# The input part of a recurrence: copied into PSUM by ScalarE in place of an identity product

## The chip, the cores and the metric

The kernel runs on one core of a Trainium2 chip. A core has TensorE (PE; its weight loads are listed apart as PEld), VectorE (DVE), ScalarE (ACT), GpSimd (POOL) and SyncE (SP), each with its own queue of instructions; they wait for each other through semaphores. Matrix products write to PSUM, which has eight banks of 512 f32 values for each of 128 partitions. The metric is the time of one execution on the device, in microseconds (us).

## What is computed

The program is a chain of graph layers and feed-forward layers over a graph of 3125 nodes with 256 features. The change lies in one of them, a recurrence over B = 1, T = 3125 steps on layer-normalised rows x:

```python
xt = jnp.swapaxes(x, 0, 1)
xi = xt @ U_i + b_i          # and xf, xg, xo
def step(carry, xs):
    h, c = carry
    xi_t, xf_t, xg_t, xo_t = xs
    i_t = jax.nn.sigmoid(xi_t + h @ V_i)
    g_t = jnp.tanh(xg_t + h @ V_c)
    o_t = jax.nn.sigmoid(xo_t + h @ V_o)
    c_new = h * c + i_t * g_t
    h_new = o_t * jnp.tanh(c_new)
    return ((h_new, c_new), h_new)
(_, _), hs = lax.scan(step, (h0, c0), (xi, xf, xg, xo))
```

The forget gate isn't used in the new cell: the old cell is multiplied by h. The layer's output is hs, and it is added to x.

## The kernel before

The method `recurrence` cuts the 3125 steps into 64 chunks of 49 (G = 2 groups, R = 32 chunks in each, L = 49 steps) and runs all chunks side by side, each from a guess of its starting state. It repeats this for ROUNDS = 5 rounds, each of which takes the chunks' starting states from the ends of the chunks before them in the round before. The first round, `round_(SKIP)`, begins at step 20 and so has 29 steps; four more rounds of 49 steps stand in a hardware loop, `For_i` (L1843). At the end a flag is set where the last two rounds still differ; any flag starts the program's second path, a general version of everything.

Before the rounds, the input part of all steps, x times U plus bias, is computed once into the SBUF tile `pre` (L1735 with target px, and L1757). One partition holds one chunk's part of one quarter of the features: 4 quarters x 32 chunks are 128 partitions, and a row of 192 values holds 64 features for each of three gates.

One step of one group is, by the names in the profile:

- L1770, `before_h`: TensorE multiplies the identity with `pre` for this step and group. This writes the input part into the PSUM tile `pz` (start=True); each group has two such tiles, in a bank each (L1760).
- L1735, `quarters`: eight products of `hist` (the transposed h of the step before, as weights) with the matrix `lstm_v`, four quarters for each of two halves of h, added in `pz`. In f32 a product is two records in the trace, so there are 16 to a step.
- L1815: ACT takes the tanh of all three gates, `z`.
- L1817 and L1821: DVE makes `ig` from z and then the new `cell`, with `hc` (h times the old cell, L1793, made a half step earlier).
- L1829: ACT takes the tanh of the cell, `tcell`.
- L1831 and L1835: DVE makes `h` and transposes it into `hist`, from which the next step's products load their weights.

The two groups are independent within a round and are written in turn, g = 0 and g = 1 for each step. A planner in the framework sets the order of instructions on each engine from its own estimates of when each is ready. `issue_after(x)` keeps what is written in its block behind x in the queue of x's engine; it adds no wait. Here it keeps each identity product behind the products of the step, those behind the previous identity product, and `hc` behind the other group's cell. The framework also places the semaphore waits. An instruction that needs more waits than it can hold gets an event-semaphore instruction ahead of it, on the same engine, for the rest.

Of the kernel before, what the change touches and what calls it, by code (L numbers as in the profile page):

```python
# [13 lines left out]
AF = mybir.ActivationFunctionType  # L14
ALU = mybir.AluOpType
AX = mybir.AxisListType
PSUM = bass.MemoryType.PSUM
# [58 lines left out]
class Net:  # L76
# [1608 lines left out]
    def recurrence(self, name, general=False):  # L1685
# [17 lines left out]
        nc, x = self.nc, self.x  # L1703
# [3 lines left out]
        G, L = GROUPS, CHUNK  # L1707
        T = G * R * L
        with ExitStack() as ctx:
# [15 lines left out]
            pre = c.tile([P, G, L, W], F32, name="pre")  # L1725
# [5 lines left out]
            def quarters(pz, stationary, moving, start, stop):  # L1731
                for q in range(Q):
                    s = stationary[q] if isinstance(stationary, list) else stationary
                    m = moving if len(moving.shape) == 2 else moving[:, q, :]
                    made = nc.tensor.matmul(  # L1735
                        pz[q * R : (q + 1) * R, :], s, m,
                        start=start, stop=stop, tile_position=(0, q * R),
                    )
                return made.ins

            with ExitStack() as inner:
                wk = self.pool(inner, name + "projwork", 3)
                xt = self.pool(inner, name + "projx", 1).tile([P, KD, NP], F32, name="xt")
                psum = self.pool(inner, name + "projps", 4, space=PSUM)
# [7 lines left out]
                for g in range(G):  # L1752
                    for s in range(L):
                        pz = psz.tile([P, W], F32, name="px", padded_shape=[P, 512])
# [2 lines left out]
                        nc.vector.tensor_add(pre[:, g, s, :], pz, bs)  # L1757
            with ExitStack() as inner:
                wk = self.pool(inner, name + "work", 3)
                psum = [self.pool(inner, f"{name}ps{g}", 2, space=PSUM) for g in range(G)]  # L1760
                pst = self.pool(inner, name + "pst", 1, space=PSUM)
                hall = c.tile([P, KD, NP], F32, name="hall")
                nc.gpsimd.memset(hall[:, :, T:], 0.0)
                nc.vector.memset(ends, 0.0)
                nc.vector.memset(start_t, 0.0)
                nc.vector.memset(hist[:, :, L - 1], 0.0)

                def before_h(g, s):
                    pz = psum[g].tile([P, W], F32, name="pz", padded_shape=[P, 512])
                    made = nc.tensor.matmul(  # L1770
                        pz, self.ident, pre[:, g, s, :], start=True, stop=False
                    )
                    return pz, made.ins

                def round_(begin=0):

                    first = wk.tile([P, 2, J], F32, name="first")
                    celt = wk.tile([P, KD, R], F32, name="celt")
                    nc.vector.tensor_copy(start_t[:, 0, :, 1:], hist[:, 1, L - 1, :, 0 : R - 1])
                    nc.vector.transpose(celt.rearrange("p k r -> p (k r)"), ends[:, 1, 1, :])  # L1780
                    nc.vector.tensor_copy(start_t[:, 1, :, 1:], celt[:, :, 0 : R - 1])
                    for i in range(2):
                        nc.vector.transpose(
                            first[:, i, :], start_t[:, i].rearrange("p k r -> p (k r)")
                        )
                    h = [first[:, 0, :], ends[:, 0, 0, :]]
                    cell = [first[:, 1, :], ends[:, 1, 0, :]]
                    ht = [start_t[:, 0], hist[:, 0, L - 1]]
                    hc = [None] * G

                    def carried(g):
                        to = wk.tile([P, J], F32, name=f"hc{g}")
                        nc.vector.tensor_mul(to, h[g], cell[g])  # L1793
                        return to


                    pz = []
                    for g in range(G):
                        tile, last = before_h(g, begin)
                        pz.append(tile)  # L1800
                    for s in range(begin, L):
                        for g in range(G):
                            with self.tc.issue_after(last):
                                for k in range(KD):
                                    made = quarters(
                                        pz[g], ht[g][:, k, :], vs[:, k], False, k == KD - 1
                                    )
                            last, following = made, None
                            if s + 1 < L:
                                with self.tc.issue_after(made):  # L1810
                                    following, last = before_h(g, s + 1)
                            if hc[g] is None:
                                hc[g] = carried(g)
                            z = wk.tile([P, W], F32, name=f"z{g}")
                            nc.scalar.activation(z, pz[g], AF.Tanh)  # L1815
                            ig = wk.tile([P, J], F32, name=f"ig{g}")
                            nc.vector.scalar_tensor_tensor(  # L1817
                                ig, z[:, 0:J], 1.0, z[:, 2 * J :], op0=ALU.add, op1=ALU.mult
                            )
                            now = wk.tile([P, J], F32, name=f"cell{g}")  # L1820
                            made = nc.vector.scalar_tensor_tensor(  # L1821
                                now, hc[g], 0.5, ig, op0=ALU.mult, op1=ALU.add
                            )
                            cell[g], hc[g] = now, None
                            if g == 0 or s + 1 < L:
                                with self.tc.issue_after(made.ins):
                                    hc[1 - g] = carried(1 - g)
                            tcell = wk.tile([P, J], F32, name=f"tcell{g}")
                            nc.scalar.activation(tcell, cell[g], AF.Tanh, scale=0.5)  # L1829
                            h[g] = wk.tile([P, J], F32, name=f"h{g}")  # L1830
                            nc.vector.scalar_tensor_tensor(  # L1831
                                h[g], z[:, J : 2 * J], 1.0, tcell, op0=ALU.add, op1=ALU.mult
                            )
                            ht[g] = hist[:, g, s]
                            nc.vector.transpose(ht[g].rearrange("p k r -> p (k r)"), h[g])  # L1835
                            pz[g] = following
                    for g in range(G):
                        for i, now in enumerate((h[g], cell[g])):
                            nc.vector.tensor_sub(moved[:, i, g, :], now, ends[:, i, g, :])
                            nc.vector.tensor_copy(ends[:, i, g, :], now)  # L1840

                round_(SKIP)
                with self.tc.For_i(0, (G * R if general else ROUNDS) - 1, 1):  # L1843
                    round_()

                halls = [
                    hall[:, k, :T].rearrange("p (b g s) -> p g s b", g=G, s=L) for k in range(KD)
                ]
                for b in range(0, R, R // 2):
                    cut = slice(b, b + R // 2)  # L1850
                    for g in range(G):
                        nc.vector.tensor_scalar(
                            halls[0][:, g, :, cut], hist[:, g, :, 0, cut], 0.5, None, op0=ALU.mult
                        )
                        nc.scalar.mul(halls[1][:, g, :, cut], hist[:, g, :, 1, cut], 0.5)

                last = wk.tile([P, 1], F32, name="last")
                nc.vector.tensor_reduce(last, self.ident[:, R - 1 :: R], AX.X, ALU.add)
                nc.vector.tensor_scalar(last, last, -1.0, 1.0, op0=ALU.mult, op1=ALU.add)
                nc.vector.tensor_mul(moved, moved, moved)  # L1860
                nc.vector.tensor_scalar(moved, moved, 4 * TOL * TOL, None, op0=ALU.is_le)
                nc.vector.tensor_scalar(moved, moved, -1.0, 1.0, op0=ALU.mult, op1=ALU.add)
                nc.vector.tensor_scalar(
                    moved[:, :, 1, :], moved[:, :, 1, :], last, None, op0=ALU.mult
                )
                count = wk.tile([P, 1], F32, name="count")
                nc.vector.tensor_reduce(count, moved, AX.XYZ, ALU.add)
                pc = pst.tile([P, 512], F32, name="pc")
                nc.tensor.matmul(pc[:1, :1], count, self.ones[:, 0:1], start=True, stop=True)
                nc.vector.tensor_copy(self.flags[:, 4:5], pc[:1, :1])  # L1870
# [940 lines left out]
```

## Time and profile before

| what | us |
|---|---|
| median of 3 runs | 4003.65 (4002.43 to 4005.65) |
| the profiled execution | 4006.18 |
| its span, first to last instruction | 4004.5 |
| projection into `pre`, L1735 into px | 1615.8 to 1681.4 |
| first round, 29 steps | 1681.4 to 1764 |
| four rounds of 49 steps | 1764 to 2343 |
| one identity product, two records | 0.59 |
| the 16 records of a step's products | 0.86 |
| `z`, 128x192 | 0.33 |
| `tcell`, 128x64 | 0.26 |

In a group's line, the number after x is the count of records, then come the busy time and the mean of one in ns, then the engine's idle time just before them and what ended most of it. In the timeline the columns are start, duration, engine, line and operation, then out<-in with the shape. Square brackets give the idle time before the instruction and what ended it. In the windows the columns are the stretch, its length, the busy time of PE, PEld, DVE, ACT and POOL with counts, the granted share of the TensorE clock, the share of the DMA engines and GB/s.

### The profile page before, as it was taken

How to read it: one execution, taken by the hardware profiler on the slowest of the kernel's cores; microseconds unless marked ns; L12 is line 12 of the kernel's file. 1: busy time of each engine (PE TensorE's matmuls, PEld its weight loads, DVE VectorE, ACT ScalarE, POOL GpSimd, SP SyncE). 2: the span in 40 equal slices, each digit the busy share in tenths (PEclk: the TensorE clock that was granted, in tenths of full speed). 3: DMA queues.
4: the chain of work that ended last, by engine and by line, in shares of the span. 5: the costliest groups of instructions: out<-in, count | busy, mean ns of one | idle time of the engine just before them, and what ended most of it. 6: DMA issues, size and time to landing. Idle time of an engine off the chain costs nothing. (4 is left out here: it accounts for less than half of the span.)

```text
span 4004.5 us, 71406 instructions
## 1 busy us (share of the span) xinstructions
PE 3505.5 (88%) x25991; PEld 2138.1 (53%) x26079; DVE 2149.8 (54%) x7762; ACT 1171.7 (29%) x3566; POOL 1422.2 (36%) x1316
## 2 busy tenths in 40 slices
PE   4776986668898798999999979999999999899898
PEld 3343222553232476745444555555566888766687
DVE  7787997447777566677666671111256211244411
ACT  2565334243333111134333441001001322220122
POOL 2777776345787375000000021111122222222243
PEclk7677997788999899999999989999999999899999
DMA  4556343553444554000000012333464444435465
GB/s 122 160 160 191 107 115 94 163 190 108 114 124 106 137 159 125 4 2 2 2 2 2 2 30 78 94 91 92 135 183 152 118 120 121 141 110 156 118 166 122
DMA packets 366365, 422.12 MB, mean 105 GB/s; under 512 B 44076, under 2 KB 320864, under 8 KB 362295
## 3 DMA queue, kind: packets, MB, share of 16 engines
q1 hardware_dynamic: 286833, 260.46, 21.8%
q0 software_dynamic: 62224, 140.41, 13.8%
q10 hardware_dynamic: 16950, 16.54, 1.3%
q8 instruction: 217, 3.56, 0.4%
q14 instruction: 141, 1.16, 0.1%
HBM read 337.37 MB, written 82.62 MB: 105 GB/s over the span
## 5 line engine op out<-in xcount | busy, mean ns | idle before, releaser
L1952 POOL DMA_INDIRECT edge<-scored,from x720 | 853.5, 1185 | 339.7 <-issue 181.2
L1735 PE MATMUL pz<-lstm_v,hist 128*32 128x192 f32 x7120 | 384.6, 334 | 31.5 <-DVE hist L1835 8.6
L1515 PE MATMUL acc<-c,hs 128*128 128x512 bf16 (+1 forms) x2070 | 406.0, 356 | 1.6
L1535 PE MATMUL acc<-hs,c 128*128 128x512 bf16 x1192 | 394.9, 379 | 0.0
L2599 PE MATMUL ph<-xt,first 128*128 128x256 f32 (+1 forms) x1624 | 350.4, 371 | 2.7 <-DMA first<-in_f_first 1.9
L2005 ACT ACTIVATE edge<-edge,factor 128x65 f32<-128x65 f32 (+1 forms) x960 | 251.4, 349 | 316.4 <-DVE factor L2000 251.9
L1539 PE MATMUL acc<-hs,c 128*128 128x256 bf16 x1250 | 340.6, 272 | 3.0
L2617 PE MATMUL py<-w,ht 128*128 x1484 | 335.8, 380 | 0.7 <-DVE y L2622 0.7
L1515 PEld LDWEIGHTS <-hs 128*128 128x128 bf16 x2100 | 205.5, 98 | 198.9
L2599 PEld LDWEIGHTS ph<-xt,first 128*128 128x128 f32 x1624 | 291.2, 197 | 38.3 <-ACT xt L2565 2.1
L2617 PEld LDWEIGHTS py<-w,ht 128*128 128x128 f32 x1484 | 282.0, 191 | 38.9 <-issue 1.0
L1735 PEld LDWEIGHTS pz<-lstm_v,hist 128*32 128x32 f32 x7120 | 186.7, 109 | 180.1 <-DVE hist L1835 147.5
L1770 PE MATMUL pz<-pre,ident 128*128 128x192 f32 x900 | 269.8, 383 | 12.2 <-PEq L1843 12.2
L1586 POOL TENSOR_TENSOR disc<-deg,expo 128x25 f32<-128x25 f32 x1 | 4.4, 4357 | 769.7 <-DVE ends L1840 769.7
L2269 POOL DMA_INDIRECT slots<-rows,sloti x150 | 164.7, 1098 | 315.2 <-DVE rstd L340 136.8
L2607 ACT ACTIVATE ht<-ph,first 128x256 f32<-128x256 f32 (+1 forms) x406 | 160.6, 455 | 310.5 <-PE ph L2599 301.6
L971 DVE SCALAR_TENSOR_TENSOR v<-q,g1ahv,c 128x384 f32<-128x384 f32 (+1 forms) x400 | 236.9, 643 | 11.1 <-PE acc L1038 11.0
L1123 PE MATMUL acc<-g1bhv,v 128*128 128x257 f32 x850 | 204.7, 396 | 14.6 <-DVE v L971 8.4
L1770 PEld LDWEIGHTS pz<-pre,ident 128*128 128x128 f32 x900 | 136.9, 191 | 150.1 <-issue 72.0
L1815 ACT ACTIVATE z<-pz 128x192 f32<-128x192 f32 x450 | 148.6, 330 | 189.9 <-PE pz L1735 164.2
L2015 PE MATMUL edgeacc<-edge,hot 128*32 128x264 f32 (+1 forms) x1440 | 142.5, 462 | 69.1 <-DVE edge L2008 34.7
L676 PE MATMUL pa<-hi,lo 128*128 128x350 bf16 (+2 forms) x600 | 163.8, 422 | 41.7 <-DVE hi L667 34.9
(532 smaller groups left out, 5426.6 us busy)
## 6 DMA issues: line engine op xcount, KB each, us to landing
c<-ct SPq DMA_DIRECT2D x103, 640.0 KB
c<-ct SPq DMA_DIRECT2D x75, 480.0 KB
first<-in_f_first SPq DMA_DIRECT2D x29, 1158.0 KB
slots<-slots SPq DMA_DIRECT2D x159, 130.0 KB
ct<-cols SPq DMA_DIRECT2D x12, 1600.0 KB
first<-in_f_first SPq DMA_DIRECT2D x29, 642.0 KB
edge<-scored,from POOLq DMA_INDIRECT x720
first<-in_f_first SPq DMA_DIRECT2D x29, 385.0 KB
```

Source lines behind the costliest of these rows:

```text
L971: nc.vector.scalar_tensor_tensor(to, q[:, h, :w], hv[:, s, h, D // nh + 1 : D // nh + 2], cols[s], op0=ALU.max, op1=ALU.mult,)
L1123: nc.tensor.matmul(a[:, : D + 1], v[0][:, j * P : (j + 1) * P], hv[:, s, 0, : D + 1], start=(s == 0), stop=(s == NT - 1),)
L1515: self.nc.tensor.matmul(acc[f][:, : n * P], lhs, cols[s], start=(s == 0 and i == 0), stop=(s == NT - 1), skip_group_check=True,)
L1535: nc.tensor.matmul(acc[t], lhs, hs[:, s, 0:2, :].rearrange("p i d -> p (i d)"), start=start, stop=stop, skip_group_check=True,)
L1539: return nc.tensor.matmul(acc[t][:, D:], lhs, hs[:, s, 2, :], start=False, stop=stop, skip_group_check=True,)
L1735: made = nc.tensor.matmul(pz[q * R : (q + 1) * R, :], s, m, start=start, stop=stop, tile_position=(0, q * R),)
L1770: made = nc.tensor.matmul(pz, self.ident, pre[:, g, s, :], start=True, stop=False)
L1952: nc.gpsimd.indirect_dma_start(out=tile[:, g, :], out_offset=None, in_=self.rows, in_offset=bass.IndirectOffsetOnAxis(ap=index, axis=0),)
L2005: nc.scalar.mul(part, part, factor[:, g, h : h + 1])
L2269: nc.gpsimd.indirect_dma_start(out=net.slot_views[(2 * t + r) % len(net.slot_views)], out_offset=bass.IndirectOffsetOnAxis(ap=self.sloti[: ...
L2599: made = nc.tensor.matmul(ph[:, m - m0, :n, :], st["w1"][:, k * hid + m * P : k * hid + (m + 1) * P], st["xt"][:, k, :n, :], start=(k == 0 ...
L2617: nc.tensor.matmul(py[:, j, :], st["ht"][:, m, j, :], st["w2"][:, m * D : (m + 1) * D], start=(m == 0), stop=(m == nhc - 1),)
```

## The change

`before_h` no longer issues a product. ACT copies the step's slice of `pre` into `pz`, and all eight products of the step are then added to it: they were already written with start=False, and get an argument that leaves out a check of groups. The copy for step s+1 is kept behind the z of step s on ACT's queue. The products no longer stand behind the identity product of the other group but behind that group's products. Each group has three PSUM tiles for `pz` in place of two. Line numbers after L1735 shift by a few in the changed file: the copy is L1771, z L1811, ig L1816, cell L1820, tcell L1828, h L1830, the transpose L1834.

```diff
                     made = nc.tensor.matmul(
                         pz[q * R : (q + 1) * R, :], s, m,
                         start=start, stop=stop, tile_position=(0, q * R),
+                        skip_group_check=True,
                     )
...
-                psum = [self.pool(inner, f"{name}ps{g}", 2, space=PSUM) for g in range(G)]
+                psum = [self.pool(inner, f"{name}ps{g}", 3, space=PSUM) for g in range(G)]
...
                     pz = psum[g].tile([P, W], F32, name="pz", padded_shape=[P, 512])
-                    made = nc.tensor.matmul(
-                        pz, self.ident, pre[:, g, s, :], start=True, stop=False
-                    )
-                    return pz, made.ins
+                    nc.scalar.copy(pz, pre[:, g, s, :])
+                    return pz
...
                     for g in range(G):
-                        tile, last = before_h(g, begin)
-                        pz.append(tile)
+                        pz.append(before_h(g, begin))
+                    last = None
                     for s in range(begin, L):
                         for g in range(G):
-                            with self.tc.issue_after(last):
+                            with self.tc.issue_after(last) if last else nullcontext():
                                 for k in range(KD):
                                     made = quarters(
                                         pz[g], ht[g][:, k, :], vs[:, k], False, k == KD - 1
                                     )
                             last, following = made, None
-                            if s + 1 < L:
-                                with self.tc.issue_after(made):
-                                    following, last = before_h(g, s + 1)
                             if hc[g] is None:
                                 hc[g] = carried(g)
                             z = wk.tile([P, W], F32, name=f"z{g}")
-                            nc.scalar.activation(z, pz[g], AF.Tanh)
+                            made = nc.scalar.activation(z, pz[g], AF.Tanh).ins
+                            if s + 1 < L:
+                                with self.tc.issue_after(made):
+                                    following = before_h(g, s + 1)
```

## The prediction

> **What bounds the kernel now.** I read the page first (which lines are costly), then the windows around the recurrence, then the timeline of two steps, then the event-semaphore rows and the granted clock. The page:
>
> ```profile
> span 4004.5 us, 71406 instructions
> L1735 PE MATMUL pz<-lstm_v,hist 128*32 128x192 f32 x7120 | 384.6, 334 | 31.5 <-DVE hist L1835 8.6
> L1770 PE MATMUL pz<-pre,ident 128*128 128x192 f32 x900 | 269.8, 383 | 12.2 <-PEq L1843 12.2
> ```
>
> The removed line shows 270 us of TensorE time, and the recurrence (1681 to 2343 us) shows TensorE about 93% busy, as in this window, one pass of the loop (columns: PE, PEld, DVE, ACT, POOL, clock, DMA):
>
> ```profile
> 1909.50:2052.90 143.40, 133.66 (x1764) 70.89 (x1764) 100.53 (x502) 57.46 (x196) 0.00 (x0) 0.99 0.01 2
> ```
>
> That share misleads. The timeline of one full step of a group (rows of the other group are between them):
>
> ```profile
> 2041.20 0.86 PE L1735 MATMUL pz<-lstm_v,hist 128*32 128x192 f32 x16
> 2041.98 0.59 PE L1770 MATMUL pz<-pre,ident 128*128 128x192 f32 x2
> 2042.18 0.33 ACT L1815 ACTIVATE z<-pz 128x192 f32<-128x192 f32 x1 [0.33 <-PE pz L1735]
> ...
> 2042.54 0.22 DVE L1817 SCALAR_TENSOR_TENSOR ig<-z 128x64 f32<-128x64 f32 x1
> 2042.80 0.22 DVE L1821 SCALAR_TENSOR_TENSOR cell<-hc,ig 128x64 f32<-128x64 f32 x1
> ...
> 2043.12 0.26 ACT L1829 ACTIVATE tcell<-cell 128x64 f32<-128x64 f32 x1 [0.61 <-DVE cell L1821]
> ...
> 2043.41 0.23 DVE L1831 SCALAR_TENSOR_TENSOR h<-z,tcell 128x64 f32<-128x64 f32 x1 [0.24 <-ACT tcell L1829]
> 2043.50 0.33 ACT L1815 ACTIVATE z<-pz 128x192 f32<-128x192 f32 x1
> 2043.74 0.24 DVE L1835 STREAM_TRANSPOSE hist<-h 128x64 f32<-128x64 f32 x1
> 2043.91 0.18 DVE L1817 SCALAR_TENSOR_TENSOR ig<-z 128x64 f32<-128x64 f32 x1
> 2044.04 0.48 PEld L1735 LDWEIGHTS pz<-lstm_v,hist 128*32 128x32 f32 x16 [0.44 <-DVE hist L1835]
> ```
>
> Start to start: products to z 0.98, z to ig 0.36, ig to cell 0.26, cell to tcell 0.32, tcell to h 0.29, h to transpose 0.33, transpose to next products 0.30: 2.85 us, all of it one group's dependences. The products start 0.05 us after the transpose ends, in both groups, so TensorE is free then. The identity product (2041.98) runs while z, ig and cell do: it is off the path.
>
> **The price of a second wait.** Early in the first round cell to tcell takes 0.25 us, not 0.32:
>
> ```profile
> 1686.47 0.23 DVE L1821 SCALAR_TENSOR_TENSOR cell<-hc,ig 128x64 f32<-128x64 f32 x1
> 1686.72 0.26 ACT L1829 ACTIVATE tcell<-cell 128x64 f32<-128x64 f32 x1 [0.55 <-DVE cell L1821]
> ```
>
> There tcell waits on one semaphore; from the eighth step on it has an extra event-semaphore instruction that carries the wait for cell: about 0.06 us. The same holds for z, and for the transpose from step 20 of a round (0.33 against 0.26). So a step takes 2.66 us in the first seven steps, 2.77 where the transpose has one wait, 2.85 where it has two.
>
> **The change, part by part.** Orders and waits below are those of the two built programs; outside the recurrence every engine's list is the same.
>
> (a) 450 identity products leave TensorE (900 records, 269.8 us). They lie beside z and the cell arithmetic; inside a step they free nothing, since the products wait for the transpose: 0.
>
> (b) 450 copies on ACT, pre to PSUM, 128x192. Nearest rows: tcell 0.26 (128x64, SBUF) and z 0.33 (128x192, out of PSUM) below, the 128x256 SBUF activation at L1204 0.41 above. Order is z, copy, tcell, with no wait on the copy in the steps. ACT idles 0.61 us between z and tcell, so even 0.41 fits: 0. If that cover were gone, each excess would come straight onto tcell.
>
> (c) Waits. tcell's event semaphore goes (-0.06). The first product of a step now waits for the transpose, an older product and the copy, and the wait for the transpose moves to an event-semaphore instruction on TensorE:
>
> ```profile
> L1770 PEldq EVENT_SEMAPHORE  x16: 51/51/51, 1761.5 to 2204.5; - x16
> ```
>
> In the trace a weight load starts 0.053 us after the releasing DVE instruction; where such an instruction carried the wait, 0.115 (L347, L505, L1876). Queued behind it are only this burst and the other group's, which comes later anyway. So +0.06. Sum with tcell: 0. Bounds: PE's could cost 0 to 0.12, that is -0.06 to +0.06 a step.
>
> (d) Order on VectorE, which the source diff doesn't show. Before: h, transpose, then the other group's ig. After, in every step but one of a round, one group (X) has h, **ig of the other group (Y), then X's transpose**. X's transpose is queued behind an instruction that waits for Y's z, and Y's z stands behind X's tcell in ACT's queue. X's cycle becomes: z to tcell 0.36+0.26+0.26 = 0.88; tcell to Y's z 0.16 (back-to-back activations overlap, row below: seven take 1.77 us, one 0.34, so the next starts about 0.10 before the end; 0.26-0.10); z to ig 0.36; ig to transpose 0.16 (as transpose to ig, 2043.74 to 2043.91); transpose to products 0.36; products to z 0.99. Sum 2.91.
>
> ```profile
> 1199.81 1.77 ACT L2005 ACTIVATE edge<-edge,factor 128x65 f32<-128x65 f32 x7
> ```
>
> Y's own cycle, with X's transpose between its ig and cell (+0.06), gives 2.84 to 2.91 and fits in. Against 2.85: +0.06; against 2.77: +0.14; against 2.66: +0.25. First round: 22 x 0.14 + 7 x 0.25 = 4.8. Four passes of 20 x 0.14 + 29 x 0.06 = 4.5: 18.2. Sum **+23 us**. Bounds: no cost at all (the ig is always early): 0. If activations don't overlap (+0.10) and ig to transpose costs as much as ig to cell (+0.10): 3.11 a step, 22 x 0.34 + 7 x 0.45 + 4 x (20 x 0.34 + 29 x 0.26) = +68. I take the middle sum: its rows are back-to-back rows of the same engines.
>
> (e) Round starts. The two identity products ahead of the first real ones run at half clock (2054.56 to 2056.14), though start_t was ready at 2054.61; two copies on ACT take about 0.6 and then the products can go: -1.2 for the first group, about -2 for the second, four times: -8. Against that, TensorE stays at half clock until enough work fills a window; now 3.4 to 6.8 us a round, then perhaps 0 to 8 windows more at 1 us of loss each; two more, +2 a round: +8. Sum 0, bounds -8 and +30.
>
> (f) Third PSUM bank per group: no row shows a wait for a bank in the steps. 0. The Trainium skill (Perfetto Trace Analysis, Matmul Optimizations) advises to use all eight banks; by that rule a gain would be expected, by this trace none.
>
> Sum: 23 + 0. The profiled execution took 4006.18 us (span 4004.5), 2.5 above the median of the runs; on the median, 4003.65 + 22 = **4026**.
>
> **Rivals.** *The clock falls* (slower by far). Without the identity products TensorE is busy 2 x 0.86 of 2.91 us, 59%, and in the thinnest 3.4 us window 2 x 0.86 = 51%. Three windows:
>
> ```profile
> 1322.40:1325.80 3.40, 2.01 (x8) 1.24 (x8) 0.29 (x2) 1.75 (x9) 0.00 (x0) 1.00 0.00 1
> 1762.80:1766.20 3.40, 1.65 (x26) 1.00 (x30) 2.43 (x14) 0.59 (x2) 0.00 (x0) 1.00 0.01 2
> 1766.20:1769.60 3.40, 2.63 (x30) 1.25 (x22) 1.60 (x9) 0.84 (x3) 0.00 (x0) 0.50 0.00 0
> ```
>
> 59% kept the full clock, 49% was followed by 0.50, and another window at 53% (1329.3) too. [...] At half clock, products to z takes 1.64 (2056.14 to 2057.78) and the two groups' products queue: 1.43 + 0.36 + 0.16 + 0.36 + 1.63 = 3.94 a step, +1.12 x 225 = +252 if it never recovers (4255); half of the time, about 4130. The Trainium skill (TensorE: Matmul & The Clock Gate, Part 1) ties half rate to an idle window of about 3.4 us; by that rule there is no such window and this rival is out, but here 1762.8 to 1766.2 was no idle window and the clock fell.
>
> *No net cost* (within the bound): Y's ig is always early enough: 3996 to 4011.
>
> *Faster*: the order on VectorE costs nothing and PE's new event wait is hidden, so tcell's 0.06 stays gained: 225 x 0.06 + 8 = -22, 3982. It decides if X's transpose starts no later than 0.33 after its h; against it stands the sum in (d).
>
> *The change doesn't act*: no row of before shows a product added to a value that ACT wrote. If the copied values were lost, instructions and durations would be the same; only the flag of unfinished rounds could then start the second path, at roughly twice the time. 2%. The Trainium skill (PSUM — Partial Sum Buffer, The four PSUM rules) states that such a product adds where an earlier product has marked the element and overwrites it elsewhere; the trace can't show the marks.
>
> **How the numbers follow.** Order on VectorE costs (4010 to 4098): 60%. Clock: 18%. No net cost: 12%. Faster: 8%. Second path: 2%. The range leaves out the faster rival, the second path and the worse half of the clock's cases: 3997 to 4130; the likeliest case alone, 4010 to 4075. A difference of 0.2% (8 us) is about what a measurement of this kernel can tell from none. Faster 0.09, same 0.14, slower 0.77.
>
> **What would show it.** In the timeline after: L1770's products gone, a copy of 0.3 to 0.4 right behind each z; cell to tcell 0.26; a TensorE event semaphore ahead of each step's first load, which starts about 0.115 after the transpose; one group's transpose directly behind the other's ig, and a step of about 2.91 in both halves of a round. A step of 2.85 or less makes (d) wrong; granted clock of 0.5 outside the round starts makes the clock the cause; an idle ACT of under 0.1 before tcell makes (b) wrong.

## The result, and the profile after

The changed kernel took 4014.52 us (median of 12 runs, 4006.18 to 4027.41), the kernel before, beside it on the same chip, 4001.96 (12 runs). The ratio is 1.0034, with a 95% interval of 1.0022 to 1.0046: slower by 0.34%, 12.6 us. Of the 22 us that the prediction added (its sum is 23), a good half came, and, as it said, the removed 270 us of TensorE time bought nothing inside a step. What it bought at the starts of the rounds is measured below.

The profiled execution took 4023.91 us, one of the longer ones. The page of the kernel after, its span and the line of the recurrence's products:

```profile
span 4022.1 us, 70147 instructions
L1735 PE MATMUL pz<-lstm_v,hist 128*32 128x192 f32 x7120 | 403.6, 347 | 258.2 <-DVE cell L1820 231.4
```

TensorE's idle time before these products rose from 31.5 to 258.2 us. What was taken from TensorE came back as waiting.

The timeline of the kernel after, one full step of the group that is late (rows between them left out):

```profile
2042.16 0.51 PEld L1735 LDWEIGHTS pz<-lstm_v,hist 128*32 128x32 f32 x16 [1.37 <-ACT pz L1771]
2043.17 0.33 ACT L1811 ACTIVATE z<-pz 128x192 f32<-128x192 f32 x1 [0.72 <-PE pz L1735]
2043.40 0.33 ACT L1771 COPY pz<-pre 128x192 f32<-128x192 f32 x1
2043.53 0.22 DVE L1816 SCALAR_TENSOR_TENSOR ig<-z 128x64 f32<-128x64 f32 x1 [0.47 <-ACT z L1811]
2043.79 0.22 DVE L1820 SCALAR_TENSOR_TENSOR cell<-hc,ig 128x64 f32<-128x64 f32 x1
...
2044.05 0.26 ACT L1828 ACTIVATE tcell<-cell 128x64 f32<-128x64 f32 x1 [0.33 <-DVE cell L1820]
2044.21 0.31 ACT L1811 ACTIVATE z<-pz 128x192 f32<-128x192 f32 x1
2044.34 0.22 DVE L1830 SCALAR_TENSOR_TENSOR h<-z,tcell 128x64 f32<-128x64 f32 x1 [0.19 <-ACT tcell L1828]
...
2044.56 0.23 DVE L1816 SCALAR_TENSOR_TENSOR ig<-z 128x64 f32<-128x64 f32 x1
2044.70 0.24 DVE L1834 STREAM_TRANSPOSE hist<-h 128x64 f32<-128x64 f32 x1
...
2045.05 0.51 PEld L1735 LDWEIGHTS pz<-lstm_v,hist 128*32 128x32 f32 x16 [1.37 <-ACT pz L1771]
```

The reader is to see the order at the end: h at 2044.34, then the other group's ig at 2044.56, and only then this group's transpose. That ig waits for the other group's z (2044.21), which stands behind this group's tcell (2044.05) on ACT. Start to start: products to z 1.01, z to ig 0.36, ig to cell 0.26, cell to tcell 0.26, tcell to the other z 0.16, to ig 0.35, ig to transpose 0.14, transpose to products 0.35: 2.89 us. The brackets name the copy, L1771, as what ended TensorE's idle time; but the copy for these products, behind this group's z of the step before, had ended at 2040.84. The wait that ended last is the transpose's.

The views of the copy's line and of the products' line in the kernel after (count, shortest, median and longest in ns):

```profile
L1771 ACT COPY pz<-pre x450: 315/325/326, 1636.0 to 2364.4; 128x192 f32<-128x192 f32 x150
...
L1735 PEldq EVENT_SEMAPHORE  x451: 51/51/51, 1620.5 to 2365.9; - x151
```

The copy takes 0.325 us and lies in ACT's idle time, which is still 0.33 us before tcell. One event semaphore now precedes each step's products.

For the comparisons I cut the recurrence by the starts in the z rows. "First" is the first round, first z to last z. A "start" goes from a round's last z to the fifth step of the next one, and "rest" from there to that round's last z; four of each are added up. Times are us.

| kernel | ratio to before (95%) | first | starts | rest | sum |
|---|---|---|---|---|---|
| before | 1 | 78.7 | 78.3 | 502.6 | 659.5 |
| after, profiled at 4023.91 | 1.0034 (1.0022 to 1.0046) | 82.1 | 74.6 | 524.0 | 680.7 |
| after again (e9) | 1.0024 (1.0009 to 1.0038) | 82.1 | 67.4 | 516.3 | 665.8 |
| e1, order undone | 0.998 (0.9968 to 0.9993) | 79.5 | 66.9 | 506.0 | 652.5 |
| e2, order undone, spare product | 0.9989 (0.9978 to 1.0) | 79.7 | 69.4 | 506.0 | 655.1 |
| e3, late order, spare product | 1.0198 (1.0181 to 1.0215) | 90.4 | 76.2 | 565.8 | 732.4 |
| e4, before with late order | 1.015 (1.013 to 1.0169) | 87.5 | 79.0 | 549.8 | 716.3 |
| e5, late order, one spare product | 1.0003 (0.9976 to 1.003) | 82.1 | 66.2 | 514.0 | 662.3 |
| e6, two banks | 1.0023 (1.0003 to 1.0043) | 82.0 | 67.8 | 515.8 | 665.6 |
| e7, before with copy | 0.9919 (0.9889 to 0.9949) | 75.6 | 72.9 | 481.3 | 629.8 |
| e8, before with small copy | 0.9919 (0.9896 to 0.9942) | 75.7 | 73.3 | 481.4 | 630.4 |
| e10, order undone, lean waits | 0.9947 (0.993 to 0.9964) | 77.9 | 65.2 | 495.7 | 638.8 |
| e11, before, lean waits | 0.9899 (0.9882 to 0.9916) | 75.7 | 73.7 | 472.3 | 621.7 |
| e12, e11 with copies at round starts | 0.9907 (0.9872 to 0.9941) | 75.7 | 70.0 | 472.3 | 618.0 |

The runs e5 to e8 and e12 fell on chips where the part of the program ahead of the recurrence took 115 to 155 us longer in the profiles; the recurrence's steps took the same there.

### The profile page after: what moved, and what is told of

It reads as the page before. It is cut to its first block, busy times and chain, and to the rows that moved or that the text cites. A ratio compares the mean times of both kernels' runs of the same rounds, so it can differ in the third digit from the quotient of the medians.

```text
span 4022.1 us, 70147 instructions
## 1 busy us (share of the span) xinstructions
PE 3301.1 (82%) x25179; PEld 2044.1 (51%) x25179; DVE 2123.1 (53%) x7762; ACT 1250.7 (31%) x4016; POOL 1421.8 (35%) x1316
## 5 line engine op out<-in xcount | busy, mean ns | idle before, releaser
L1735 PE MATMUL pz<-lstm_v,hist 128*32 128x192 f32 x7120 | 403.6, 347 | 258.2 <-DVE cell L1820 231.4
L1735 PEld LDWEIGHTS pz<-lstm_v,hist 128*32 128x32 f32 x7120 | 232.8, 114 | 428.9 <-ACT pz L1771 310.0
L1535 PE MATMUL acc<-hs,c 128*128 128x512 bf16 x1250 | 411.2, 379 | 0.0
L971 DVE SCALAR_TENSOR_TENSOR v<-q,g1ahv,c 128x384 f32<-128x384 f32 (+1 forms) x400 | 236.5, 642 | 11.4 <-PE acc L1038 11.2
L1811 ACT ACTIVATE z<-pz 128x192 f32<-128x192 f32 x450 | 145.3, 323 | 181.9 <-PE pz L1735 179.1
L1031 PE MATMUL acc<-v,g1ahv 128*64 128x384 f32 (+1 forms) x800 | 179.7, 557 | 26.0 <-DVE v L971 25.1
L1535 PEld LDWEIGHTS <-c 128*128 128x128 bf16 x1250 | 126.0, 101 | 136.6
```

The lines of the kernel that those rows point to most:

```text
L971: nc.vector.scalar_tensor_tensor(to, q[:, h, :w], hv[:, s, h, D // nh + 1 : D // nh + 2], cols[s], op0=ALU.max, op1=ALU.mult,)
L1031: made = nc.tensor.matmul(acc[h // 2][r : r + HC, :w], hv[:, s, h, :HC], v[h], start=first, stop=last, tile_position=(0, r),).ins
L1535: nc.tensor.matmul(acc[t], lhs, hs[:, s, 0:2, :].rearrange("p i d -> p (i d)"), start=start, stop=stop, skip_group_check=True,)
L1735: made = nc.tensor.matmul(pz[q * R : (q + 1) * R, :], s, m, start=start, stop=stop, tile_position=(0, q * R), skip_group_check=True,)
```

## The experiments

**Is it the order on VectorE?** e1 undoes that one thing in the kernel after: ig is kept behind the other group's transpose.

```diff
-                            nc.vector.scalar_tensor_tensor(
-                                ig, z[:, 0:J], 1.0, z[:, 2 * J :], op0=ALU.add, op1=ALU.mult
-                            )
+                            with self.tc.issue_after(turned) if turned else nullcontext():
+                                nc.vector.scalar_tensor_tensor(
+                                    ig, z[:, 0:J], 1.0, z[:, 2 * J :], op0=ALU.add, op1=ALU.mult
+                                )
...
-                            nc.vector.transpose(ht[g].rearrange("p k r -> p (k r)"), h[g])
+                            turned = nc.vector.transpose(
+                                ht[g].rearrange("p k r -> p (k r)"), h[g]
+                            ).ins
```

> The kernel after, with each ig held behind the other group's transpose: only the order on VectorE goes back to h, transpose, ig. Theory (the order sets the step): step 2.71 to 2.84 us instead of 2.89, the later products start 0.11 after the transpose; 225 x 0.05 to 0.13 = 11 to 29 us below after, minus what a half clock after the round starts costs, so 3990 to 4006 us against 4002 of before. Rival (TensorE's new event wait or the copy sets the step): the step stays at 2.89 and the time at 4014. Rival (the half clock after round starts is the whole loss): the warm step is 2.89 or not, but the time stays above 4010 wherever the half clock lasts more than 7 us in a round.

It took 3997.97 us against 4004.64 of before: 0.998. The step is 2.79, and 2.87 from step 20 on, where the transpose has two waits. The timeline of e1:

```profile
2042.01 0.23 DVE L1831 SCALAR_TENSOR_TENSOR h<-z,tcell 128x64 f32<-128x64 f32 x1 [0.19 <-ACT tcell L1829]
2042.18 0.33 ACT L1811 ACTIVATE z<-pz 128x192 f32<-128x192 f32 x1 [0.20 <-PE pz L1735]
2042.34 0.24 DVE L1835 STREAM_TRANSPOSE hist<-h 128x64 f32<-128x64 f32 x1
...
2042.54 0.23 DVE L1817 SCALAR_TENSOR_TENSOR ig<-z 128x64 f32<-128x64 f32 x1
2042.70 0.51 PEld L1735 LDWEIGHTS pz<-lstm_v,hist 128*32 128x32 f32 x16 [1.01 <-ACT z L1811]
```

The transpose comes 0.33 after its h, ahead of the ig. Against after's undisturbed execution (e9) the first round and the rests are 2.6 and 10.3 us shorter: 12.9 us is the order's price. What is left over before, 0.9 in the first round and 3.4 in the rests, is 0.02 a step: TensorE's event semaphore and a slightly later z, less the one that tcell no longer has. The expected step, 2.71 to 2.84, held but for the steps from 20 on in the four later rounds; that the ratio is below 1 is the work of the starts, which are 11.4 us shorter than before.

**Does the missing TensorE work cost clock?** e2 and e3 give TensorE an identity product again, into a PSUM tile that nobody reads: e2 in the order of e1, e3 in the late order of the kernel after (group 0's transpose behind group 1's ig).

```diff
+                            with self.tc.issue_after(made):
+                                made = nc.tensor.matmul(
+                                    spare, self.ident, pre[:, g, s, :], start=True, stop=True
+                                ).ins
                             last, following = made, None
```

> The same order, and behind each group's products one spare product of pre with the identity into a PSUM tile that nobody reads: extra work that keeps TensorE as full as in the kernel before, with the copy and the waits of after. Theory (order plus half clock): half clock of 3.4 to 6.8 us at each round start and a narrow spread of times, 0 to 15 us below the run without the spare product, 3985 to 4000 us. Rival (clock plays no part): as the run without the spare product, within 4 us.

e2: 4000.52, ratio 0.9989, 2.6 us more than e1 between the first and last z, all in the starts, and with as wide a spread (3989.95 to 4008.09; e1 3985.37 to 4005.91). The theory, 0 to 15 us below e1 and a narrow spread, failed. In this order the clock plays no part that the spare product could mend; the rival held.

> The kernel after with its order on VectorE kept (one group's transpose behind the other's ig) and the spare product added: only the clock is changed against after. Theory: half clock of at most 7 us a round, step 2.89; the order alone is left, 4003 to 4011 us against 4002 of before and 4014 of after, and the spread of the runs is under 8 us where after has 21. Rival (the order costs nothing, the clock everything): 3990 to 4002. Rival (the clock costs nothing): 4014.

e3: 4081.7 us, ratio 1.0198. No theory expected that. And e4, which puts the same late order into the kernel before, missed in the same way:

```diff
-                            nc.vector.scalar_tensor_tensor(
+                            made = nc.vector.scalar_tensor_tensor(
                                 ig, z[:, 0:J], 1.0, z[:, 2 * J :], op0=ALU.add, op1=ALU.mult
                             )
+                            if g == 1:
+                                with self.tc.issue_after(made.ins):
+                                    nc.vector.transpose(
+                                        ht[0].rearrange("p k r -> p (k r)"), h[0]
+                                    )
...
-                            nc.vector.transpose(ht[g].rearrange("p k r -> p (k r)"), h[g])
+                            if g == 1:
+                                nc.vector.transpose(ht[g].rearrange("p k r -> p (k r)"), h[g])
```

> The kernel before with group 0's transpose issued behind group 1's ig, as the kernel after has it: the order alone, with the identity products and the waits of before. Theory: the step rises from 2.66/2.77/2.85 to about 2.88, 22 x 0.11 + 7 x 0.22 in the first round and 20 x 0.11 + 29 x 0.03 in each of four more: 12 to 20 us slower than before. Rival (the order is free and the copy or the new wait on TensorE is the cause): within 4 us of before.

4061.45 us, 1.015, with a step of 3.09 (3.18 in e3). The timeline of e4 shows why:

```profile
2040.83 0.86 PE L1735 MATMUL pz<-lstm_v,hist 128*32 128x192 f32 x16 [0.40 <-DVE hist L1822]
...
2041.60 0.24 DVE L1841 STREAM_TRANSPOSE hist<-h 128x64 f32<-128x64 f32 x1
...
2041.62 0.59 PE L1770 MATMUL pz<-pre,ident 128*128 128x192 f32 x2
...
2042.14 0.48 PEld L1735 LDWEIGHTS pz<-lstm_v,hist 128*32 128x32 f32 x16 [0.23 <-issue]
```

The second group's transpose ends at 2041.84, its products start at 2042.14: 0.30 later, not 0.05. They stand behind the identity product, which follows the first group's products. In the kernel before, the two groups' products start 1.32 and 1.52 us apart in turn (2041.20, 2042.52, 2044.04), and products and identity product (0.79 and 0.53 from one start to the next) just fit in between. In the late order they start 1.01 apart (2042.16 and 2043.17 in the kernel after), and the second group pays. So the identity product is off the path only in the old order; in the new one its absence keeps the price at 2.89 a step, where 3.09 to 3.18 would be due.

e5 therefore puts the spare product behind group 1's products alone (the diff of e3 with `if g == 1`), where TensorE waits anyway.

> The kernel after with its late transpose (group 0's behind group 1's ig) and a spare product into an unread PSUM tile behind group 1's products alone, where TensorE of after stands idle for about a microsecond until group 0's transpose: it fills TensorE without standing ahead of the other group's products. Theory (order and clock): step 2.89, half clock at most 7 us a round, so after's warm loss of 2.5 to 2.7 us a round alone: 4003 to 4011 us against 4002 to 4005 of before, and a spread of under 14 us where after has 21. Rival (half clock has no part in the loss): 4014 and a spread of 20. Rival (any product ahead of the next burst is paid in the late order): step 3.0 or more, 4035 or more.

The step stayed at 2.89, the half clock at 3.4 us in three starts and none in the first; 662.3 us, 3.5 less than after again. Its ratio, 1.0003 (0.9976 to 1.003), is too wide to set it apart from after's 1.0034. And since e6 and e9 had no long half clock either, without a spare product, e5 doesn't show that the product prevents one.

**The third bank.** e6 is the kernel after with two PSUM tiles per group (`3` back to `2` in the pool of `pz`).

> The kernel after with two PSUM banks per group instead of three. Theory (the third bank is worth nothing): step 2.89, 4006 to 4022 us like after's 4014. Rival (the third bank lets the copy go early): the copy waits for the older products, the step rises by up to the wait: above 2.95 a step, 4028 or more.

Step 2.89, ratio 1.0023 (1.0003 to 1.0043): as after. The third bank is worth nothing, as predicted. The Trainium skill (Perfetto Trace Analysis, Matmul Optimizations) advises to have all eight PSUM banks in use; here, six for `pz` in place of four gained nothing.

**The half clock.** The profiled execution of after has something that no other profile showed: in the last two rounds TensorE stays at half clock for 37.6 and 34.1 us after the start, and a step takes 3.79. The windows of the kernel after, each 3.41 us long, from that stretch (columns as before: stretch, length, PE, PEld, DVE, ACT, POOL, clock, DMA):

```profile
2059.09:2062.50 3.41, 0.86 (x16) 0.50 (x16) 3.00 (x18) 0.84 (x3) 0.00 (x0) 1.00 0.02 5
2062.50:2065.91 3.41, 1.66 (x24) 1.08 (x28) 1.12 (x7) 0.60 (x3) 0.00 (x0) 0.50 0.01 2
...
2069.33:2072.74 3.41, 2.52 (x32) 1.58 (x32) 1.59 (x9) 1.37 (x6) 0.00 (x0) 0.50 0.00 0
...
2082.98:2086.39 3.41, 2.40 (x36) 1.29 (x32) 1.90 (x10) 1.62 (x6) 0.00 (x0) 0.50 0.00 0
...
2093.22:2096.63 3.41, 2.55 (x32) 1.34 (x24) 1.66 (x9) 1.37 (x6) 0.00 (x0) 0.50 0.00 0
2096.63:2100.05 3.42, 2.79 (x32) 1.57 (x32) 1.53 (x9) 1.44 (x6) 0.00 (x0) 0.50 0.00 0
2100.05:2103.46 3.41, 1.72 (x33) 1.03 (x35) 2.42 (x14) 1.70 (x8) 0.00 (x0) 1.00 0.00 0
```

The clock falls behind the change of rounds (0.86 us busy, 25%). Here the nine windows that are 70 to 77% busy at half clock leave it there, and the one that reaches 82% ends it. The other runs show that the busy time of a window doesn't settle it. The first line is e5's fourth start, 76% busy, with full clock behind it; the other two are e11's first start, where identity products ran: 91% busy, and half clock for a further window.

```profile
2332.11:2335.52 3.41, 2.60 (x32) 1.43 (x32) 1.61 (x9) 1.21 (x5) 0.00 (x0) 0.50 0.02 5
...
1762.27:1765.68 3.41, 3.11 (x27) 1.49 (x30) 1.90 (x10) 0.89 (x5) 0.00 (x0) 0.50 0.00 0
1765.68:1769.10 3.42, 3.42 (x31) 1.51 (x24) 1.06 (x6) 0.73 (x4) 0.00 (x0) 0.50 0.00 0
```

If in the kernel after a window does have to be about that full, the length of the stretch can be estimated. A cold step of 3.79 us shifts by 0.38 against the windows, so it can take nearly ten of them (3.79 / 0.38) until one holds two groups' products nearly whole: some 34 us. That this is the reason isn't shown. e9 is the kernel after once more.

> The kernel after once more, for the half clock. Theory (the half clock ends with the first 3.41 us window that is at least about 80% busy, and a cold step of 3.79 us puts only 70 to 77% into most windows, so the end comes only where a window meets nearly two bursts): stretches between 3.4 and 38 us, different from round to round and from run to run; warm steps 2.89 everywhere. If all four rounds recover within 7 us, first z to last z is 662 to 667 us, and the warm loss of 2 to 3 us a round is all there is; each long stretch adds about 7. Rival (the stretch is a property of the round): the third and fourth pass again cold for 34 to 38 us.

4011.8 us, ratio 1.0024, and no stretch beyond 6.8 us; 665.8 us from first to last z, inside the expected 662 to 667. So the long stretch is no property of the round. Per-run clocks point the same way: of the 24 runs of after in both series, the nine with a mean clock of 0.921 or less (a line drawn afterwards) have a median of 4023.1 us, the other fifteen 4009.7. The 13 us between them are near the 15 that the two profiles differ by. That is a correlation: only one execution with long stretches was profiled, and what decides where a round meets the windows wasn't tried.

**What a second wait costs.** e7 adds to the kernel before a copy of the next step's `pre` to an unread PSUM tile, behind z; e8 the same with 8 columns.

```diff
-                            nc.scalar.activation(z, pz[g], AF.Tanh)
+                            made = nc.scalar.activation(z, pz[g], AF.Tanh).ins
+                            if s + 1 < L:
+                                with self.tc.issue_after(made):
+                                    nc.scalar.copy(spare, pre[:, g, s + 1, :])
```

> The kernel before with an extra copy of the next step's pre to a PSUM tile that nobody reads, behind each z on ACT; products and the order on VectorE as before. The waits change: tcell waits for VectorE alone and z for TensorE alone. Theory (the copy of 0.33 us is hidden, an event semaphore costs 0.06 on the path): steps 2.71 and 2.78 instead of 2.77 and 2.85, 225 x 0.06 = 14 us below before, 3986 to 3994. Rival (the copy holds up tcell or the transposes): step at or above before's, 4002 or more.

> As the run with the extra copy, but of 8 columns instead of 192: the change of waits with next to none of the copy's work. Theory (copy hidden): the same time as with the wide copy within 4 us, 3986 to 3994. Rival (the wide copy's work costs): at least 4 us below the wide copy.

Both 0.9919: the copy's work is hidden, as theory said, but the gain was some twice the expected one (659.5 to 629.8 us from first to last z in e7). The copy takes the wait for ACT's own last write upon itself, so z loses its event semaphore too (products to z 0.92 in place of 0.98), not tcell alone. The step is 2.65, and 2.73 from step 20 on, against 2.77 and 2.85: twice 0.06. The event semaphores of z in the kernel before, and in e7, where the one that is left stands ahead of the first round:

```profile
L1815 ACTq EVENT_SEMAPHORE  x441: 17/17/67370, 1615.8 to 2342.7; - x147
...
L1816 ACTq EVENT_SEMAPHORE  x1: 66767/66767/66767, 1745.2 to 1745.2; - x1
```

That repaired the theory, and two more runs tried it. e10 gives z the same relief in e1, with a copy of 8 columns of z to an unread tile:

```diff
                                     following = before_h(g, s + 1)
+                                    nc.scalar.copy(spare[:, 0:8], z[:, 0:8])
```

> The kernel after with transposes ahead of ig, and behind each copy a further copy of 8 columns of z to a PSUM tile that nobody reads, which takes the wait for ACT's own z upon itself, so that z waits for TensorE alone. Theory (a second wait costs 0.06 on the path; the small copy is hidden): steps 2.73 and 2.81 instead of 2.79 and 2.87 with the order alone, 225 x 0.06 = 13 us less, 0.994 to 0.996 of before. Rival (the waits are free): 0.998 of before, as with the order alone.

3985.83 us, 0.9947 (0.993 to 0.9964), steps 2.73 and 2.81, all as expected. In e11, at a round's end, VectorE reads the last products' PSUM tiles (`done` holds each group's last `pz`) once in e8, so that the later transposes need no wait for TensorE:

```diff
+                    seen = wk.tile([P, G], F32, name="seen")
+                    for g in range(G):
+                        nc.vector.tensor_copy(seen[:, g : g + 1], done[g][:, 0:1])
```

> The kernel before with the small extra copy on ACT, and at the end of each round two one-column copies on VectorE out of the last products' PSUM tiles, so that the transposes of the later steps need no wait for TensorE. Theory (each second wait costs 0.06 to 0.08 on the path): the step is 2.65 in all steps of all rounds; against the run with the small copy alone 4 x 29 x 0.07 = 8 us less, against before 39 us less: 0.989 to 0.991 of before. Rival (the copies at the round's end are paid): as with the small copy alone, 0.992.

3964.05 us against 4004.23: 0.9899 (0.9882 to 0.9916), 40 us faster than before and 48 faster than after in the same series (4011.8), with the identity products in place. The windows of e11, and its transposes, which have no event semaphore left (before has 229):

```profile
2080.00:2120.00 40.00, 40.00 (x542) 21.62 (x542) 31.85 (x151) 19.79 (x91) 0.00 (x0) 1.00 0.01 2
```

```profile
L1840 DVE STREAM_TRANSPOSE hist<-h x450: 236/245/247, 1684.2 to 2306.0; 128x64 f32<-128x64 f32 x150
```

At 2.65 a step TensorE shows no gap any more: products and identity products of both groups take 2 x (0.79 + 0.53) = 2.64. But one group's dependences add up to as much. From its products at 2080.49, z comes 0.92 later, then ig 0.36, cell 0.27, tcell 0.26, h 0.28, the transpose 0.26 and the next products, at 2083.14, 0.30: 2.65. So by this sum, which no run tries, taking the identity products away wouldn't shorten this step either.

**The round starts.** e12 is e11 with after's ACT copies for the first step of each round alone.

```diff
-                        tile, last = before_h(g, begin)
+                        tile = psum[g].tile([P, W], F32, name="pz", padded_shape=[P, 512])
+                        nc.scalar.copy(tile, pre[:, g, begin, :])
```

> The lean kernel before (small copy on ACT, two one-column copies at a round's end), and the first input part of each group in a round copied into PSUM by ACT as in the kernel after; the identity products stay in all other steps. Theory (the copies' gain lies at the round starts alone, where the identity products run at half clock): from a round's last z to the fifth step of the next 73.7 us become 65 to 68 in the four starts together, the step stays at 2.65; 6 to 9 us less than the lean kernel, 0.987 to 0.989 of before. Rival (the starts of after are short for another reason): 0.990 of before, starts 73 or more.

The four starts take 70.0 us, 3.7 less than e11's 73.7, where 6 to 9 were expected: part of after's short starts, but not all. In three of the four the first step still takes 4.4 to 4.7 us, as identity products at half clock stand between its products. The ratio, 0.9907 (0.9872 to 0.9941), can't be told from e11's.

## Why the prediction was right, and where it was off

Slower was right, and for the reason that it gave; 4014.5 lies in the range. The signs that it named for the likeliest case are in the trace: the copy behind z, cell to tcell 0.26, an event semaphore ahead of the products, these 0.11 after the transpose's end, the other group's ig ahead of the transpose, and a step of 2.89. By its steps:

- **(a) identity products, 0.** Right for the old order. It missed that in the late order they cost 0.2 to 0.3 a step (e4 and e3, against 2.89). No number of the sum changes, since its cycle was reckoned without them.
- **(b) copy, 0.** Right: 0.325 us, hidden (e7 against e8).
- **(c) and (d) waits and order, +23.** The mechanism held, row by row. Of the 23, 16 steps in the starts stand apart (16 x 0.14 = 2.2), so 20.8 compare with what was measured in the first round and the rests without a long half clock: 3.45 + 13.71 = 17.2. The cycle came out at 2.89 and not 2.91 (ig to transpose 0.14 for 0.16, transpose to products 0.35 for 0.36), 0.02 x 209 = 4.2, a little more than the difference of 3.6. A smaller slip lies in the rows of before: 2.66 holds for the first two steps of the first round, the third takes 2.72 and from the fourth on it is 2.77, so seven steps at +0.25 were some 0.5 us too many. By e1, 12.9 of the 17.2 are the order, 4.3 the balance of the waits, which (c) had put at 0.
- **(e) round starts, -8 and +8, sum 0.** This was the mis-sized term. The starts gained 10.9 us in e9, and with 16 steps that are 0.12 longer in them, nearer 13: the first z comes 2.02 us after the round's first instruction of TensorE or ACT (2063.87 to 2065.89) in place of 3.22 (2054.56 to 2057.78), and the first steps at half clock no longer have identity products between them. In e9 the half clock is short, and its cost lies inside these starts; in the recorded profile it cost about 15 us more. So the sum is 17.2 - 10.9 = 6.3 us, plus 0 to 15; the medians, +12.6 and +7.6, lie in that.
- **(f) third bank, 0.** Right (e6).

The direction is owed to the mechanism, but the size in part to luck: without long half clock stretches the sum is 6.3 us, less than a third of 22, and inside what the rival of no net cost allowed.

Of the rivals, the clock came true in small: 0.5 outside the round starts, the sign that the prediction named for it, was there for eleven windows and for ten, not for the whole recurrence. A cold step took 3.79, where 3.94 was reckoned. The faster rival was to decide if X's transpose starts within 0.33 of its h: in after it is 0.36 (2044.34 to 2044.70), in e1 0.33, and e1 is on the faster side. The prediction went by how busy a warm window is before the clock falls, and had falls behind 49% and 53%; in the kernel after windows that are 50% busy kept the clock all through the rounds, and the loss came only behind a change of rounds. What it lacked is the other side: what a cold window needs to get it back, which stays open. The Trainium skill (TensorE: Matmul & The Clock Gate, Part 1) has the clock return after a busy window of about 3.4 us and fall after an idle one. In the kernel after's trace the window before the fall held 0.86 us of products, and nine windows 70 to 77% busy didn't bring the clock back.

## What to carry to other kernels

Work that is off the path can still set an order: before taking it out, see where the planner puts everything else then, and hold the order that matters by hand; here that one line was worth 13 us and turned the sign. In a chain of small dependent instructions, count the waits of each: every second wait of z, tcell and the transpose was worth 0.06 to 0.08 us on the path, where the removed product was worth nothing in the order of before, and an instruction off the path can take one over. A share of 93% busy on an engine said nothing of what its work costs; the gap between its groups of work, against their length, did.

## What was not expected of the hardware

- TensorE's clock, once halved, stayed halved in the kernel after through nine windows of 3.41 us that were 70 to 77% busy, and came back after one at 82%, in the next round after one at 78%. That with a period near the window's length (3.79 against 3.41) the return waits for the two to line up is an inference from this one execution. Busy time alone doesn't decide: 2.75 us (80%) was followed by 0.50 once and by 1.00 elsewhere, 2.60 us in e5 by 1.00, 3.11 us in e11 by 0.50.
- An event semaphore is 17 ns on ACT, 21 on VectorE and 51 on TensorE in the records, but between the instructions on their two sides those on ACT and VectorE cost 0.06 to 0.08 us (z 0.98 to 0.92, the step 2.73 to 2.65 without the transpose's), TensorE's 0.05 to 0.06 (transpose to products 0.30 to 0.35 and 0.36).
